# A fixed order of seven slots to a step, and attention by 32x32 tiles summed in PSUM

## The chip, the cores and the metric

The kernel runs on one core of one Trainium2 chip. A core has TensorE (matrix products, into PSUM), VectorE, ScalarE and GpSimd (element-wise work and reductions) and SyncE, which here issues nearly all DMA transfers. Each engine works through its own list of instructions in order and waits on semaphores for the others. The metric is the device time of one execution in microseconds (us), given as the median of several runs. One execution is also recorded by the hardware profiler; its page and trace are what is read below. In the profile PE is TensorE's matmuls, PEld its weight loads, DVE VectorE, ACT ScalarE, POOL GpSimd, SP SyncE, and a trailing q an engine's sequencer.

## What is computed

The input `x` is 4 x 4096 rows of 512 values in fp32. Three residual stages follow each other:

```python
x = x + 0.5 * ffn(layernorm(x))          # first half
x = x + attention(layernorm(x))          # neighbourhood attention
x = x + 0.5 * ffn(layernorm(x))          # second half, same weights
```

`ffn` is one 512 x 512 linear layer whose input and weight are first quantised in blocks of 32 values: each block is scaled so that its largest magnitude is 7.5 and rounded to the nearest of a six-bit grid. The attention has 16 heads of 32 values. Each query sees the 13 keys around it (fewer offsets at the ends of a sequence, where the window is shifted):

```python
qkv = x @ qkv_w.T + qkv_b                       # q is scaled by 32 ** -0.5
attn = softmax(q . k[neighbours] + rpb[offset]) # 13 scores a query and head
out = (attn . v[neighbours]) @ proj_w.T + proj_b
```

## The kernel before

**Precision.** fp32 products are made from fp16 halves: each operand is a rounded high part and a low part, and the helper `product` (L148-160) sums three groups of matmuls, high x low, low x high and high x high, with four pieces of the contraction each: 12 matmuls of 128x128 weights on 512 columns. An FFN or output product has one more, for the bias (L152).

**Stages of a row tile.** A tile `t` has 128 rows (128 tiles in all). It is loaded (`load`), normalised and quantised (`quantised_norm(t, "n1")`, L187-205), multiplied (`ffn`, L214-221), normalised again (`layernorm`, L170-185), transposed by DMA into `x2`, and its values are computed and written to HBM (`values`, L235-249). The row statistics and the scale factors go over VectorE and GpSimd, `nbn` (L183) on VectorE. Splitting and transposing is in `transposed` (L207-212): ScalarE makes the high half, VectorE the low one, SyncE issues the transposing DMA. After the attention `project_out` (L460-469) multiplies, adds the residual and starts the third norm ("n3"), and `second_half` (L471-473) does the last FFN and stores the tile.

**Stages of an attention item.** An item `m` is four heads (one of four pieces `c` of 128 channels) of a group of four tiles, 512 rows; there are 128 items. Queries are cut into blocks of 30, whose neighbourhoods cover 42 keys; a group has 16 to 18 blocks, 2192 blocks in all over the items. `project_qk` (L280-318) makes queries and keys (2 x 12 matmuls), keeps the last 42 positions of each item in `halo` for the next group (two VectorE copies), and copies each head's queries into a block-diagonal tile `bd`, one copy per head and half (VectorE for three heads, ScalarE for one). `softmax` (L343-399) then needs two matmuls a block, both with 128x128 weights from `bd` (the first gives scores against the high and the low keys at once, 84 columns, the second those of the low queries, 42 columns):

```python
nc.tensor.matmul(o, bd[:, 0, i, :], keys, start=True, stop=False)
nc.tensor.matmul(o[:, 0, :], bd[:, 1, i, :], keys[:, 0, :], start=False, stop=True)
```

The two sets of scores lie apart in PSUM. VectorE adds the bias table to the first (L377) and then the second to that (L380). Then come the maximum (VectorE), its subtraction (GpSimd), the exponential (ScalarE), the sum and its reciprocal (VectorE), the scaling (GpSimd), the split into halves (L394-396) and the transposing DMA into `pT` (L398). `attend` (L401-458) makes one matmul a block, 126x128 weights from the value stack `vs` on 120 columns (four heads of 30 queries); only a quarter of the result is wanted, so ScalarE picks the four heads' pieces out of PSUM into a tile `a` (L445, twelve instructions an item), then copies the high half into `ring` (L454), and VectorE makes the low half (L455). The value stack is loaded from HBM by `load_stack`, for two items at a time.

**What sets the order.** `run_step` (one step for each tile and item, L482-520) calls the stages in a fixed sequence with their offsets in steps, `attend` at a raised priority (`AHEAD`). A scheduler then decides the place of each instruction on each engine from estimated durations and priorities. The setup (weights quantised, split and transposed, bias table) is interleaved with the first four steps. In the last steps (`ending`) work of GpSimd goes to VectorE.

Of the kernel before, what the change touches and what calls it, by code (L numbers as in the profile page):

```python
# [35 lines left out]
P = 128  # L37
# [5 lines left out]
ROWS = 4 * QN  # L43
# [4 lines left out]
PSB = 6  # L48
VB = 8
# [9 lines left out]
AHEAD = 150  # L59
# [6 lines left out]
def macaron_kernel(  # L66
# [27 lines left out]
    ps_m = ctx.enter_context(tc.tile_pool(name="ps_m", bufs=3, space=PSUM))  # L94
    ps_s = ctx.enter_context(tc.tile_pool(name="ps_s", bufs=1, space=PSUM))
    ps_v = ctx.enter_context(tc.tile_pool(name="ps_v", bufs=1, space=PSUM))
    xp = ctx.enter_context(tc.tile_pool(name="xp", bufs=15))
# [30 lines left out]
    table = const.tile([ROWS, 3, KC, KN], F32, name="table")  # L128
# [32 lines left out]

    xs, ys = {}, {}
    ending = False
# [6 lines left out]
    def layernorm(t, which):  # L170

        st = sm.tile([P, 6], F32, tag=f"st{which}", name=f"st{which}_{t}")
        nc.vector.bn_stats(st, xs[t])  # L173
        mv = sm.tile([P, 2], F32, tag=f"mv{which}", name=f"mv{which}_{t}")
        nc.vector.bn_aggr(mv, st)  # L175
        rs = sm.tile([P, 1], F32, tag=f"rs{which}", name=f"rs{which}_{t}")
        nc.gpsimd.tensor_scalar(  # L177
            rs, mv[:, 1:2], XS ** -2, LN_EPS * XS ** -2, ALU.mult, ALU.add
        )
        nc.gpsimd.tensor_tensor(rs, rs, minus_half, ALU.pow)  # L180
        y = yp.tile([P, dim], F32, tag=f"y{which}", bufs=2 if which == "n1" else 1, name=f"y{which}_{t}")
        nb = sm.tile([P, 1], F32, tag=f"nb{which}", name=f"nb{which}_{t}")
        nc.vector.scalar_tensor_tensor(nb, mv[:, 0:1], -1.0, rs, ALU.mult, ALU.mult)  # L183
        nc.scalar.activation(y, xs[t], AF.Identity, bias=nb, scale=rs)  # L184
        return y

    def quantised_norm(t, which):  # L187

        y = layernorm(t, which)
# [8 lines left out]
        eng = nc.vector if ending else nc.gpsimd  # L198
        eng.tensor_tensor(yb, yb, bc(r, QB), ALU.mult)  # L199
        q8 = q8p.tile([P, dim], F8, tag=f"q8{which}", name=f"q8_{which}_{t}")  # L200
        nc.scalar.activation(q8, y, AF.Identity, bias=nudge, saturate=False)  # L201
        eng.tensor_tensor(yb, blocks(q8), bc(sc, QB), ALU.mult)  # L202
        xT = xtp.tile([P, 2, KC, P], F16, tag=f"xT{which}", name=f"xT{which}_{t}")
        transposed(y, xT.rearrange("p s c q -> p (s c) q"), which, t)
        ys[t] = xT

    def transposed(y, dst, which, t):  # L207

        hl = hlp.tile([P, 2, dim], F16, tag=f"hl{which}", name=f"hl{which}_{t}")
        nc.scalar.copy(hl[:, 0, :], y)  # L210
        nc.vector.tensor_tensor(hl[:, 1, :], y, hl[:, 0, :], ALU.subtract)  # L211
        nc.sync.dma_start_transpose(out=dst, in_=hl.rearrange("p s k -> p (s k)"))

    def ffn(t, which):  # L214
# [5 lines left out]
        )  # L220
        nc.vector.scalar_tensor_tensor(xs[t], pm, cf, xs[t], ALU.mult, ALU.add)  # L221

    def first_half(t):

        ffn(t, "f1")
        y = layernorm(t, "n2")
        g, i = divmod(t, GROUP)
        if i == 0:
            x2[g] = x2p.tile([P, 2, KC, GROUP, P], F16, tag="x2", name=f"x2_{g}")
        transposed(y, x2[g][:, :, :, i, :].rearrange("p s c q -> p (s c) q"), "n2", t)  # L230
# [4 lines left out]
    def values(t):  # L235
# [7 lines left out]
        product(pm, lambda s, c: xg[:, s, c, i, :], lambda s, c: wt[:, s, c, VO : VO + dim])  # L243
        vt = vtp.tile([P, 2, dim], F16, tag="vt", name=f"vt{t}")
# [14 lines left out]
    def kind(j):  # L259
        return 1 if j == 0 else 2 if j == n_blocks - 1 else 0  # L260

# [18 lines left out]
    def project_qk(m):  # L280
# [5 lines left out]
        if g > 0:  # L286
            nc.vector.tensor_copy(t[:, :, :, :KN], halo[:, c])
        for s in (0, 1):
            pm = ps_m.tile([P, GT], F32, tag="mm", name=f"pmqk{s}_{m}")
            o = (QO, KO)[s] + c * P  # L290
# [4 lines left out]
            )  # L295
            bias = qk_b[:, s, c : c + 1]
            nc.scalar.activation(t[:, s, 0, KN:], pm, AF.Identity, bias=bias)
            nc.vector.scalar_tensor_tensor(  # L298
                t[:, s, 1, KN:], pm, bias, t[:, s, 0, KN:], ALU.add, ALU.subtract
            )  # L300
        if g + 1 < NG:
            nc.vector.tensor_copy(halo[:, c], t[:, :, :, GT:])
        if c == KC - 1:
            del x2[b * NG + g]

        j0, j1 = group_blocks[g]
        regular = j1 - j0 - (1 if j1 == n_blocks else 0)
        at = KN + j0 * QN - g * GT
        for h in range(4):
            rows = slice(h * D, (h + 1) * D)  # L310
            (nc.scalar.copy if h == 0 else nc.vector.tensor_copy)(  # L311
                bd[rows, :, :regular, h * QN : (h + 1) * QN],
                t[rows, 0, :, at : at + regular * QN].rearrange("p s (n q) -> p s n q", q=QN),
            )
            if j1 == n_blocks:
                nc.vector.tensor_copy(
                    bd[rows, :, regular, h * QN : (h + 1) * QN], t[rows, 0, :, KN + GT - QN :]
                )
# [24 lines left out]
    def softmax(m):  # L343
# [6 lines left out]
        ps = ps_s.tile([P, 3, 2, 256], F32, tag="s", name=f"ps{m}")  # L350
        for i in range(n):
            k0 = KN + span(j0 + i)[1] - g * GT
            u, w = divmod(i, PSB)
            o = ps[:, u, :, w * KN : (w + 1) * KN]
            keys = t[:, 1, :, k0 : k0 + KN]
            nc.tensor.matmul(o, bd[:, 0, i, :], keys, start=True, stop=False)
            nc.tensor.matmul(o[:, 0, :], bd[:, 1, i, :], keys[:, 0, :], start=False, stop=True)

        def pieces(i, e):

            while i < e:
                u, w = divmod(i, PSB)
                whole = max((e - i) // PSB, 1) if w == 0 else 1
                f = min(e, (u + whole) * PSB)
                yield slice(u, u + whole), slice(w, w + (f - i) // whole)
                i = f

        sf = sfp.tile([ROWS, MAXB, KN], F32, tag="sf", name=f"sf{m}")
        s4 = sf.rearrange("p (u w) k -> p u w k", w=PSB)
        p4 = ps[:ROWS, :, :, : PSB * KN].rearrange("p u a (w k) -> p a u w k", k=KN)  # L370
        first = 1 if kind(j0) == 1 else 0
        last = n - (1 if kind(j1 - 1) == 2 else 0)
        for i, e in ((0, first), (first, last), (last, n)):
            for u, w in pieces(i, e):
                o = s4[:, u, w, :]
                bias = table[:, kind(j0 + i), c, :].unsqueeze(1).unsqueeze(1).to_broadcast(o.shape)
                nc.vector.tensor_tensor(o, p4[:, 0, u, w, :], bias, ALU.add)  # L377
        for u, w in pieces(0, n):
            o = s4[:, u, w, :]
            nc.vector.tensor_tensor(o, o, p4[:, 1, u, w, :], ALU.add)  # L380
        s = sf[:, :n, :]
        top = sm.tile([ROWS, MAXB], F32, tag="top", name=f"top{m}")
        nc.vector.tensor_reduce(top[:, :n], s, AX.X, ALU.max)
        eng = nc.vector if ending else nc.gpsimd
        eng.tensor_tensor(s, s, bc(top[:, :n], KN), ALU.subtract)  # L385
        nc.scalar.activation(s, s, AF.Exp, scale=alpha[:ROWS])
        total = sm.tile([ROWS, MAXB], F32, tag="total", name=f"total{m}")
# [3 lines left out]
        eng.tensor_tensor(s, s, bc(total[:, :n], KN), ALU.mult)  # L391
        p = p_tile
        ph = p[:ROWS, :n, :KN]
        nc.scalar.copy(ph, s)  # L394
        nc.vector.tensor_copy(p[:ROWS, :n, 2 * KN : KV], ph)
        eng.tensor_tensor(p[:ROWS, :n, KN : 2 * KN], s, ph, ALU.subtract)
# [4 lines left out]
    def attend(m):  # L401
# [7 lines left out]
        a = ap.tile([P, MAXB * QN], F32, tag="a", name=f"a{m}")  # L409
        for i0 in range(0, n, VB):  # L410
            i1 = min(i0 + VB, n)
            k = i1 - i0
            pv = ps_v.tile([P, 2, 512], F32, tag="v", name=f"pv{m}_{i0}")
            for i in range(i0, i1):
                u, w = divmod(i - i0, VB // 2)
                nc.tensor.matmul(  # L416
                    pv[:, u, w * ROWS : (w + 1) * ROWS], st[:KV, i, col : col + P], pT[:KV, i, :ROWS],
                    start=True, stop=True,
                )
            full = k == VB  # L420
            assert full or k <= VB // 2
            pieces = [(i0, i1, 0)]
            if j1 == n_blocks and i1 == n:
                assert not full
                pieces = [(i0, n - 1, 0)] if n - 1 > i0 else []
                pieces.append((n - 1, n, n_blocks * QN - length))
            for h in range(4):
                rows = slice(h * D, (h + 1) * D)
                for e0, e1, skip in pieces:
                    w0 = e0 - i0  # L430
                    if full:
                        src = pv[rows, :, : VB // 2 * ROWS].rearrange(
                            "p u (w r) -> p u w r", r=ROWS
                        )[:, :, :, h * QN : (h + 1) * QN]
                        dst = a[rows, e0 * QN : e1 * QN].rearrange(
                            "p (u w q) -> p u w q", u=2, q=QN
                        )
                    else:
                        src = pv[rows, 0, w0 * ROWS : (w0 + e1 - e0) * ROWS].rearrange(
                            "p (w r) -> p w r", r=ROWS  # L440
                        )[:, :, h * QN + skip : (h + 1) * QN]
                        dst = a[rows, e0 * QN : e1 * QN - skip].rearrange(
                            "p (w q) -> p w q", q=QN - skip
                        )
                    nc.scalar.activation(dst, src, AF.Copy, scale=1.0 / PS)  # L445
        t0 = b * length + j0 * QN
# [378 lines left out]
```

## Time and profile before

| | |
|---|---|
| Median of 3 runs | 2903.63 us (2900.07 to 2906.81) |
| Profiled execution | 2901.23 us, its span 2899.4 us |
| VectorE busy | 2514.7 us, 87% of the span, 5212 instructions |
| TensorE busy | 2464.3 us, 85%, 16195 matmuls |
| ScalarE busy | 1821.8 us, 63%, 3570 |
| GpSimd busy | 1447.8 us, 50%, 1675 |
| Mean busy share of the 16 DMA engines, 1000-2000 us | 0.65, 123 GB/s |
| Mean granted TensorE clock | 0.955 of full speed |

The time of an engine is the time in which at least one of its instructions was running. Durations of matmuls overlap, since they are pipelined, so the distance between two starts says more than the mean duration. The page's groups give, for each line of the kernel, the operation, its tiles and shapes, the count, the busy time and mean of one, and after a bar the idle time of the engine just before it with what ended that.

### The profile page before, as it was taken

Reading aid. Unit: us, or ns where it says so; the run is one execution under the profiler, and the core shown is the slowest. Engines: PE = TensorE matmul, PEld = TensorE weight load, DVE = VectorE, ACT = ScalarE, POOL = GpSimd, SP = SyncE. Lnnn points to the kernel's source line nnn. Section 1 sums busy time; section 2 is a strip of 40 time slices with the busy share of each in tenths; the row PEclk is TensorE's granted clock in tenths of the full one; section 3 lists DMA queues with packets and bytes.
Section 4 is the critical chain, followed back from the end, with each engine's and each line's share of the span. In section 5 each row is a group of like instructions: output and inputs, shape, how many; then the busy total and the mean of one; then the engine's idle time right before and its main releaser. Section 6 shows DMA issues by size and latency. Waiting matters only on the chain.

```text
span 2899.4 us, 47348 instructions
## 1 busy us (share of the span) xinstructions
PE 2464.3 (85%) x16195; PEld 1217.8 (42%) x16195; DVE 2514.7 (87%) x5212; ACT 1821.8 (63%) x3570; POOL 1447.8 (50%) x1675
## 2 busy tenths in 40 slices
PE   1689998889898889888888888889888888888997
PEld 0244444444444434444444444344444444444443
DVE  8788988998889988888888988898888898889896
ACT  4466666666666666666665666566666566666664
POOL 5344554555455555555554555455555454545540
PEclk9899999999999999999999999999999999999998
DMA  7756765765765766766667665666666766658663
GB/s 199 161 96 121 132 124 113 137 127 110 136 127 117 136 123 120 133 119 121 132 125 124 122 123 112 127 120 121 129 121 124 126 122 126 119 110 143 127 110 78
DMA packets 931326, 362.01 MB, mean 125 GB/s; under 512 B 722830, under 2 KB 893706, under 8 KB 931084
## 3 DMA queue, kind: packets, MB, share of 16 engines
q1 hardware_dynamic: 931024, 358.98, 64.7%
q8 instruction: 127, 2.08, 0.3%
q14 instruction: 115, 0.94, 0.1%
q10 hardware_dynamic: 60, 0.01, 0.0%
HBM read 113.81 MB, written 67.27 MB: 62 GB/s over the span
## 4 chain that ended last, share of the span: by engine, by line
DVE 41%; DMA 25%; PE 11%; issue 9%; POOL 7%; ACT 6%; SPq 2%; DVEq 0%; POOLq 0%; ACTq 0%
DMA x<-in_L_attn_x_dram 9%; DVE bd L311 6%; DVE hln L211 5%; PE pmf L157 5%; DMA out_dram<-x 5%; DMA pT<-p 5%; DMA xTn<-hln 4%; DVE qk L298 4%; DVE scn L192 3%; DVE stn L173 3%; DVE x L221 2%; ACT a L445 2%; DVE scn L193 2%; DVE nbn L183 2%; POOL yn L202 2%
## 5 line engine op out<-in xcount | busy, mean ns | idle before, releaser
L157 PE MATMUL pmf<-wt,xTn 128*128 128x512 f16 x3072 | 755.0, 394 | 87.4 <-DMA xTn<-hln 82.0
L157 PE MATMUL pmqk<-x,wt 128*128 128x512 f16 x3072 | 725.8, 386 | 19.2 <-DVE vt L246 12.1
L184 ACT ACTIVATE yn<-x,nbn,rsn 128x512 f32<-128x512 f32 x384 | 310.2, 811 | 420.5 <-DVE nbn L183 412.8
L445 ACT ACTIVATE a<-pv 32x240 f32<-32x240 f32 (+2 forms) x1536 | 456.7, 301 | 136.0 <-PE pv L416 121.0
L157 PEld LDWEIGHTS <-xTn 128*128 128x128 f16 x3072 | 304.2, 101 | 481.4 <-DMA xTn<-hln 95.9
L157 PEld LDWEIGHTS <-wt 128*128 128x128 f16 x3072 | 300.5, 99 | 374.6 <-issue 48.1
L177 POOL TENSOR_SCALAR rsn<-mvn 128x1 f32<-128x1 f32 x384 | 112.1, 292 | 656.4 <-DVE mvn L175 517.1
L157 PE MATMUL pmv<-wt,x 128*128 128x512 f16 x1536 | 370.4, 392 | 34.3 <-DMA x<-hln 34.2
L173 DVE BATCH_NORM_STATS2 stn<-x 128x6 f32<-128x512 f32 x384 | 264.2, 689 | 136.1 <-DMA x<-in_L_attn_x_dram 131.8
L211 DVE TENSOR_TENSOR hln<-yn,hln 128x512 f16<-128x512 f32 x384 | 334.2, 871 | 46.4 <-ACT hln L210 45.5
L157 PE MATMUL pmo<-wt,ring 128*128 128x512 f16 x1536 | 369.0, 383 | 4.9 <-ACT ring L454 4.9
L199 POOL TENSOR_TENSOR yn<-yn,rn 128x512 f32<-128x512 f32 x248 | 269.9, 1092 | 187.1 <-DVE rn L197 135.6
L210 ACT CAST hln<-yn 128x512 f16<-128x512 f32 x384 | 236.4, 616 | 153.2 <-POOL yn L202 106.7
L416 PE MATMUL pv<-pT,vs 126*128 126x120 f16 x2192 | 183.3, 222 | 159.4 <-DMA pT<-p 126.9
L202 POOL TENSOR_TENSOR yn<-q_n,scn 128x512 f32<-128x512 fp8e4 x248 | 277.5, 1126 | 72.9 <-ACT q_n L201 72.9
L385 POOL TENSOR_TENSOR sf<-sf,top 120x714 f32<-120x714 f32 (+2 forms) x126 | 181.1, 1437 | 232.9 <-DVE mvn L175 108.1
L391 POOL TENSOR_TENSOR sf<-sf,total 120x714 f32<-120x714 f32 (+2 forms) x126 | 178.8, 1419 | 195.2 <-DVE total L390 125.1
L201 ACT ACTIVATE q_n<-yn,nudge 128x512 fp8e4<-128x512 f32 x256 | 184.0, 720 | 127.0 <-POOL yn L199 119.6
L221 DVE SCALAR_TENSOR_TENSOR x<-pmf,coef,x 128x512 f32<-128x512 f32 x256 | 184.9, 726 | 78.5 <-PE pmf L157 76.7
L416 PEld LDWEIGHTS <-vs 126*128 126x128 f16 x2192 | 144.7, 100 | 234.0 <-issue 150.9
L311 DVE COPY bd<-qk 32x1020 f16<-32x1020 f16 (+2 forms) x384 | 235.2, 612 | 7.6
L180 POOL TENSOR_TENSOR rsn<-rsn,minus_half 128x1 f32<-128x1 f32 x384 | 217.4, 566 | 30.7
(126 smaller groups left out, 3847.1 us busy)
## 6 DMA issues: line engine op xcount, KB each, us to landing
vs<-vd SPq DMA_DIRECT2D x144, 357.0 KB
x<-in_L_attn_x_dram SPq DMA_DIRECT2D x128, 256.0 KB
vd<-vt SPq DMA_DIRECT2D x128, 256.0 KB
out_dram<-x SPq DMA_DIRECT2D x128, 256.0 KB
vs<-vd SPq DMA_DIRECT2D x24, 378.0 KB
vs<-vd SPq DMA_DIRECT2D x24, 315.0 KB
xTn<-hln SPq DMA_TRANSPOSE x256
norm_of<-in_L_attn_qkv_w_dram SPq DMA_DIRECT2D x12, 256.0 KB
```

The costliest lines, as they stand in the source:

```text
L157: nc.tensor.matmul(pm, lhs(a, c), rhs(b, c), start=(n == 0), stop=(n == last))
L173: nc.vector.bn_stats(st, xs[t])
L180: nc.gpsimd.tensor_tensor(rs, rs, minus_half, ALU.pow)
L184: nc.scalar.activation(y, xs[t], AF.Identity, bias=nb, scale=rs)
L199: eng.tensor_tensor(yb, yb, bc(r, QB), ALU.mult)
L202: eng.tensor_tensor(yb, blocks(q8), bc(sc, QB), ALU.mult)
L210: nc.scalar.copy(hl[:, 0, :], y)
L211: nc.vector.tensor_tensor(hl[:, 1, :], y, hl[:, 0, :], ALU.subtract)
L221: nc.vector.scalar_tensor_tensor(xs[t], pm, cf, xs[t], ALU.mult, ALU.add)
L311: (nc.scalar.copy if h == 0 else nc.vector.tensor_copy)(bd[rows, :, :regular, h * QN : (h + 1) * QN], t[rows, 0, :, at : at + regular * QN ...
L416: nc.tensor.matmul(pv[:, u, w * ROWS : (w + 1) * ROWS], st[:KV, i, col : col + P], pT[:KV, i, :ROWS], start=True, stop=True,)
L445: nc.scalar.activation(dst, src, AF.Copy, scale=1.0 / PS)
```

## The change

The queue orders, the form of the attention and some places of work change; the computation of the 75 large matmuls of a step stays as it is.

*Order.* The stages become generators. A table of slots holds what begins when; `yield n, rank` in a stage says that its next part belongs `n` slots later, at that rank within the slot. The program is written slot by slot under `manual_schedule`, in which each engine keeps the written order. A step is seven slots. `run_step`, `AHEAD` and `ending` go away; the whole setup is written ahead of the slots. PSUM buffers for large products become four instead of three, buffers of `x` 19 instead of 15.

```diff
+    slots = {}
+    def begin(slot, stage, rank=5):
+        slots.setdefault(slot, []).append((rank, stage))
+    def run_slot(slot):
+        for _, stage in sorted(slots.pop(slot, ()), key=lambda e: e[0]):
+            for n, rank in stage:
+                begin(slot + n, stage, rank)
+                break
...
+    STEP = 7
+    F1, V, QK, SC, PV, OUT, F2 = 6, 2 * STEP + 1, 5 * STEP + 3, 6 * STEP + 5, 8 * STEP + 5, 13 * STEP + 2, 15 * STEP
...
+    for t in range(NT):
+        k = t * STEP
+        begin(k - 15, one(load, t), 0)
+        begin(k - 5, quantised_norm(t, "n1"), 1)
+        begin(k + F1, first_half(t))
+        begin(k + V, values(t))
+        begin(k + OUT, project_out(t))
+        begin(k + F2, second_half(t))
+    for m in range(n_items):
+        k = m * STEP
+        begin(k + QK, project_qk(m))
+        begin(k + SC, softmax(m), 6)
+        begin(k + PV, attend(m))
...
+        begin(k + 6 * STEP, one(load_stack, b, g, 0), 9)
+        begin(k + 8 * STEP, one(load_stack, b, g, 1), 9)
```

So within a step the slots hold, in turn: f2; values; output; queries; keys; `pv` and then the scores; f1. A norm's parts (statistics, factors, normalising, scales, first product on GpSimd, rounding, second product, high half, low half with its transposing DMA) stand in one slot each, nine in all, and the product that needs the transpose three slots after the last.

*Scores.* `bd` goes away. Each head's queries and keys are read where they lie, on the 32 partitions of the head; a matmul has weights of 32x32 and 42 columns, and writes the 32 partitions of its head. The three products of halves are summed in PSUM, so one addition of the table is left. The rows of a block become 32 for 30 queries.

```diff
-            nc.tensor.matmul(o, bd[:, 0, i, :], keys, start=True, stop=False)
-            nc.tensor.matmul(o[:, 0, :], bd[:, 1, i, :], keys[:, 0, :], start=False, stop=True)
+            for k, (a, e) in enumerate(((0, 1), (1, 0), (0, 0))):
+                for h in range(4):
+                    rows = slice(h * D, (h + 1) * D)
+                    nc.tensor.matmul(
+                        ps[rows, u, w * KN : (w + 1) * KN],
+                        t[rows, 0, a, q0 : q0 + QR], t[rows, 1, e, k0 : k0 + KN],
+                        start=k == 0, stop=k == 2,
+                    )
...
-            nc.vector.tensor_tensor(o, o, p4[:, 1, u, w, :], ALU.add)
```

*Values.* Each head has a matmul of its own, 126x32 weights on 30 columns, which writes the head's 32 partitions; the results of an item lie side by side in PSUM and are read as they are. The tile `a` goes away.

```diff
+            for h in range(4):
                 nc.tensor.matmul(
-                    pv[:, u, w * ROWS : (w + 1) * ROWS], st[:KV, i, col : col + P], pT[:KV, i, :ROWS],
+                    pv[h * D : (h + 1) * D, u, w * QN : (w + 1) * QN],
+                    st[:KV, i, col + h * D : col + (h + 1) * D],
+                    pT[:KV, i, h * QR + r : h * QR + r + QN],
                     start=True, stop=True,
                 )
...
-                    nc.scalar.activation(dst, src, AF.Copy, scale=1.0 / PS)
...
-            nc.scalar.copy(rh, piece)
-            nc.vector.tensor_tensor(ring[:, 1, c, r : r + e - t0], piece, rh, ALU.subtract)
+            nc.scalar.activation(
+                ring[:, 0, c, r : r + k], pv[:, u, at : at + k], AF.Copy, scale=1.0 / PS
+            )
+            nc.vector.scalar_tensor_tensor(
+                ring[:, 1, c, r : r + k], pv[:, u, at : at + k], 1.0 / PS, ring[:, 0, c, r : r + k],
+                ALU.mult, ALU.subtract,
+            )
```

*Places of work.* The two `halo` copies move from VectorE to ScalarE, `nbn` from VectorE to GpSimd; the last steps keep GpSimd's work on GpSimd.

```diff
-            nc.vector.tensor_copy(t[:, :, :, :KN], halo[:, c])
+            nc.scalar.copy(t[:, :, :, :KN], halo[:, c])
-        nc.vector.scalar_tensor_tensor(nb, mv[:, 0:1], -1.0, rs, ALU.mult, ALU.mult)
+        nc.gpsimd.tensor_scalar(nb, mv[:, 0:1], rs, -1.0, ALU.mult, ALU.mult)
```

## The prediction

> **What bounds the kernel now.** I read the engine shares first, then the long groups, then the chain of waits, and last the order of time inside one burst of attention.
>
> ```profile
> PE 2464.3 (85%) x16195; PEld 1217.8 (42%) x16195; DVE 2514.7 (87%) x5212; ACT 1821.8 (63%) x3570; POOL 1447.8 (50%) x1675
> ...
> DVE 41%; DMA 25%; PE 11%; issue 9%; POOL 7%; ACT 6%; SPq 2%; DVEq 0%; POOLq 0%; ACTq 0%
> ...
> L311 DVE COPY bd<-qk 32x1020 f16<-32x1020 f16 (+2 forms) x384 | 235.2, 612 | 7.6
> ```
>
> Two engines are nearly full. The chain that ended last runs 41% on VectorE and 25% on transfers, 11% on TensorE: now one, now the other is late. The third line is work that serves only the form of the attention: the block-diagonal copy of the queries, 235.2 us of VectorE.
>
> What does TensorE need? In 1500-1523 us twelve products in a row take 2.75 us with the last counted at its own 0.38, so 2.37 / 11 = 0.2155 us from start to start. A step has 75 of 512 columns (13 + 13 for the two FFNs, 12 values, 24 queries and keys, 13 output): 75 x 0.2155 = 16.16 us. The attention's are in the order of time:
>
> ```profile
> 1521.70 0.53 PE L416 MATMUL pv<-pT,vs 126*128 126x120 f16 x7
> 1522.06 0.20 PE L356 MATMUL ps<-qk,bd 128*128 128x84 f16 x1
> 1522.11 0.18 PE L357 MATMUL ps<-qk,bd 128*128 128x42 f16 x1
> 1522.13 0.20 PE L356 MATMUL ps<-qk,bd 128*128 128x84 f16 x1
> ...
> 1522.82 0.20 PE L356 MATMUL ps<-qk,bd 128*128 128x84 f16 x1
> ```
>
> The first column is the start, the second the duration, which overlaps the next. From 1522.06 to 1522.82 lie 12 blocks of two matmuls: 63 ns a block; in the trace's nanoseconds 36.5 for the 84 columns and 25.5 for the 42. A value product (0.53 us for seven, the last at 0.22) is 51.5 ns. With 2192 / 128 = 17.1 blocks a step that is 17.1 x (62 + 51.5) = 1.94 us. So TensorE needs 18.1 us of a step; the stretch 1000-2000 us holds 5782 matmuls, 126.5 a step, so a step takes 21.9. VectorE is busy for 868 of those 1000 us.
>
> **The change, part by part.**
>
> *VectorE.* Gone, by their groups' busy times: `bd` copies 235.2 + 15.4, the second addition of the scores 127 (63.4 + 29.7 + 29.1 + 5.1), the two halo copies 62.5 + 37.6 (to ScalarE), `nbn` 99.2 (to GpSimd): 577 us. The subtraction for `ring` now reads PSUM in about as many pieces (117 us stay). 2514.7 - 577 = 1938 us, 15.1 us a step. It stops being the bound as long as a step is longer.
>
> *ScalarE* loses `bd` (132), most of `a` (457) and gets 224 halo copies (37.6 + 62.5 on VectorE, up to twice that here): below 1400 us. *GpSimd* gets 384 small operations of about 292 ns (the row of L177): 112 us, some 1580 in all. Both hide under TensorE; their cover goes only if a step falls below 12.4 us.
>
> *TensorE.* The 75 products stay. The order of the built program shows, in each step, output, queries and keys, `pv`, `ps`, f1, f2, values. A block becomes 3 x 4 score matmuls of 32x32 on 42 columns and 4 value matmuls of 126x32 on 30 columns: 16 for 3, each with its own weight load, 274 pairs a step. No row of the trace has a tile of 32 columns. Bounds: if the four heads' tiles run side by side and each is as long as the 42-column matmul, 25.5 / 4 = 6.4 ns a pair; if loading and running one tile fill 25.5 each and nothing overlaps, 51 ns. In between stand 51 / 4 = 12.75 (a tile's load and run in sequence, four tiles side by side) and 25.5 (no tile beside another, loads hidden as now). I take 12.75: consecutive heads use other rows of the array and other rows of PSUM, and the trace does show a load hidden under another matmul; but 25.5 is the row nearest to it and is my first rival. 274 x 12.75 ns = 3.49 us.
>
> A skill rule speaks against it: "TensorEngine Tiling (Array Packing)", Instruction Overhead, puts about 60 cycles on every matmul however few its columns, and advises against tiling a dimension that is small; the 25.5 ns of 42 columns, where 84 take 36.5, agree with such a floor. By it the attention would be 274 x 25 ns = 6.9 us (estimate). "TensorE: Matmul & The Clock Gate", Part 3, has matmuls on different tiles start about 4 ns apart, which no run here shows; by that it would be 1.1 us (estimate).
>
> Between `pmqk`, `pv`, `ps` and f1 the form of the matmuls changes three times. If each lets the array run empty, it costs duration less spacing of a 512-column matmul, 379 - 216 = 163 ns: 0.49 us. Bounds 0 and 3 x 0.38 = 1.1.
>
> *Waits.* Each engine's order is now fixed, so whatever stands behind a waiting TensorE instruction waits with it: a late `pT` holds `ps` and all products of the next step, and through them every eviction. A slot is about 20 / 7 = 2.9 us. From the transpose of n1 or n3 to its product lie three slots (8.7 us), from that of `p` to `pv` four (11.6). The longest transposes on the chain of before took 5 to 11.5 us from issue to what they released. Stack loads go out at the end of a slot, ahead of the transposes of `p`. SyncE issues per step x 0.35, three transposes 1.25 each, `p` 2.9, values 0.58, output 0.35, a quarter of 12 stack loads at 0.45: 9.3 us, so it keeps up; and 19 x buffers let the load go 12 slots after the store that frees its buffer (before: 102.8 us of waits for that). I take 0.2 us a step for late transfers; bounds 0 and 2 (a transfer of 10.7 us against 8.7, every step). TensorE's code grows from 32,383 instructions to 89,375, 548 of a step's 700 in one burst; the page's instruction queue moved 16 KB at a time, 127 times, which is one per 256 of them. Two such pieces per burst of 3.5 us are new. Their cost is within the same bound.
>
> *Ends.* Before, TensorE had worked 9.0 + 46.1 us by 145 us, and 49.4 of the last 69.4: 110 us lost. Now the weights stand ahead of nearly all tiles, and a step holds all seven products only after 15. In the first 5.4 steps only f1 and values run: VectorE needs 6.1 us (n1 3.0, f1 0.73, n2 1.73, values 0.68) to TensorE's 25 x 0.2155 = 5.4, so 4 us are lost; and the last tile's n3 passes alone through 12 slots, some 13 us by its operations' durations (0.2 to 1.1 us) and one transpose. 110 + 17 = 127 (bounds 90 and 200).
>
> *Sum.* 16.16 + 3.49 + 0.49 + 0.2 = 20.34 us a step, x 128 = 2604, + 127 = 2731; with the 1.8 us around the profiled span (2901.23 to 2899.4) 2733, taken as **2730** against 2901.23. That run lies 2.4 us under the median of 2903.63, below what can be told apart (0.2% is about what a measurement of this kernel can tell from no change).
>
> **Rivals.**
>
> 1. *Tiles one after another.* 25.5 ns a pair: 6.99 us, a step of 23.84, 3051 + 127 + 2 = 3180. For it: the floor visible at 42 columns. Against: there each matmul covers all rows. It decides from 17.6 ns a pair: (2899.4 - 127) / 128 = 21.66, less 16.85, is 4.81 us for 274. This is the slower side.
> 2. *Fully side by side*, 6.4 ns: 1.75 us, a step of 18.6, 2510; VectorE at 15.1 of 18.6 with dependences would add half a microsecond a step, 2570.
> 3. *Fixed order meets late transfers or late code*: the full 2 us a step, 22.15 x 128 + 129 = 2964. For it: DMA is 25% of the chain and its share of 0.65 rises with shorter steps. Against: three and four slots of room.
> 4. *Load and run in sequence, no overlap*, 51 ns: 13.97 us, a step of 30.8, about 4070. Against: LDWEIGHTS hides at every matmul of before.
>
> That the order isn't what the slots say is excluded by the built order.
>
> **How the numbers follow.** Forecast 0.42 (own range 2640 to 2880: 9 to 17 ns), rival 2 0.20, rival 1 0.20, rival 3 0.10, rival 4 0.08. Faster: 0.42 + 0.20 with nearly all of both, 0.62; within 0.2% 0.03 (between forecast and rival 3); slower 0.35. The range leaves out rival 4, the upper part of rival 1 and the lowest of rival 2: 2540 to 3200.
>
> **What would show it.** Right: VectorE at 1900-2000 us busy, `bd`, `a` and the second addition gone, TensorE ending the chain; `ps` 32x42 starting 10 to 15 ns apart; TensorE's waits for `pT` and `xTn` below 30 us together. Wrong at the tile price: bursts of `pv` and `ps` of 7 us instead of 3.5. Wrong at the waits: idle TensorE of 1 us and more in most steps ahead of `pv` or `pmf`, or gaps inside a burst with nothing that released it, at every 256th instruction. Wrong at VectorE: its share still near 87% while TensorE's falls.

## The result, and the profile after

The changed kernel takes 3227.67 us (median of 4 runs, 3218.85 to 3231.78), the kernel before 2902.01 beside it: a ratio of 1.1115, 95% interval 1.1087 to 1.1144. It is slower by 11%, where 6% faster was forecast; the time lies above the range. The profiled execution has a span of 3223.1 us.

First the page of the changed kernel: engines, the granted clock in 40 slices (tenths), the queue that brings TensorE's code, the chain, and three groups of TensorE. The same two lines, clock and queue, of the kernel before stand behind it.

```profile
PE 2661.6 (83%) x44684; PEld 1295.9 (40%) x44691; DVE 2073.3 (64%) x3957; ACT 1291.0 (40%) x2178; POOL 1567.9 (49%) x2081
...
PEclk9888989988898998998989999898998889889987
...
q8 instruction: 349, 5.72, 0.8%
...
PE 82%; issue 14%; DMA 2%; DVE 1%; POOL 0%; ACT 0%; SPq 0%; ACTq 0%; DVEq 0%; POOLq 0%
...
L156 PE MATMUL pmf<-wt,xTn 128*128 128x512 f16 x3072 | 928.3, 465 | 110.2 <-DMA xTn<-hln 67.7
...
L156 PE MATMUL pmqk<-x,wt 128*128 128x512 f16 x3072 | 683.9, 379 | 0.0
...
L407 PE MATMUL ps<-qk 32*32 32x42 f16 x26304 | 258.2, 184 | 373.8 <-issue 373.8
```

```profile
PEclk9899999999999999999999999999999999999998
...
q8 instruction: 127, 2.08, 0.3%
```

VectorE fell to 64% as planned and left the chain; TensorE ends it alone. But 14% of the chain is "issue", time in which nothing that the profile shows was waited for, and 373.8 us of such idle time stand before the score matmuls. And two groups with the same operation and shape differ: a product for the queries takes 379 ns, one for the FFN 465.

The order of time of one step shows both (start, duration, and in brackets the idle time before):

```profile
1516.25 0.69 PE L472 MATMUL pv<-pT,vs 126*32 126x30 f16 x68
1516.87 1.71 PE L407 MATMUL ps<-qk 32*32 32x42 f16 x190
1522.28 0.32 PE L407 MATMUL ps<-qk 32*32 32x42 f16 x14 [3.69 <-issue]
1522.53 0.61 PE L151 MATMUL pmf<-ffn_bias,ones 128*128 128x512 bf16 x1
1522.93 1.48 PE L156 MATMUL pmf<-wt,xTn 128*128 128x512 f16 x3
```

68 value and 190 score matmuls start within 2.2 us, some 8 ns apart. Then TensorE stands for 3.69 us in the middle of a block, between matmuls that depend on nothing new, and finishes the last 14. The bias matmul after that takes 0.61 us instead of 0.38: the trace records half the clock from 1519.9 to 1526.7 us.

Where the 324 us come from: a step takes 23.66 us instead of 21.90 (both from 1000 to 2000 us), which is 225 us in 128 steps; the other 99 lie at the ends. By step:

| TensorE in a step, us | forecast | measured |
|---|---|---|
| 75 products at full clock | 16.16 | 16.16 |
| 274 small matmuls | 3.49 | 2.2 (8.0 ns each) |
| three changes of form | 0.49 | 0.32 (0.093 + 0.105 + 0.12) |
| idle stretch in the scores | within 0.2 for all waits | 3.1 (130 distances over 0.5 us from start to start, 397 us) |
| products at half clock | - | 1.8 (mean spacing 241 ns instead of 216) |
| sum | 20.34 | 23.6 |

The idle stretches have an address. I counted TensorE's instructions from the start of the trace: between 400 and 3000 us lie 124 idle stretches over 0.26 us (111 in the scores, 13 in the FFN product right behind them), and all 124 end at the same place in the count, 189 or 190 past a multiple of 256. Within a burst the place varies: the stretches in the scores come after 73 to 211 of the burst's score matmuls. The queue named "instruction" moves 349 packets of 16 KB, one for each 256 of the 89,375 instructions, and the last packet before TensorE went on had begun 2.2 to 3.4 us earlier (median 2.5). No two of its packets begin less than 3.2 us apart, in any kernel of this study; in the kernel before, the closest two are 10.3 us apart.

### The profile page after: what moved, and what is told of

Same layout as the page of the kernel before. It is cut to its first block, busy times and chain, and to the rows that moved or that the text cites. A ratio compares the mean times of both kernels' runs of the same rounds, so it can differ in the third digit from the quotient of the medians.

```text
span 3223.1 us, 101741 instructions
## 1 busy us (share of the span) xinstructions
PE 2661.6 (83%) x44684; PEld 1295.9 (40%) x44691; DVE 2073.3 (64%) x3957; ACT 1291.0 (40%) x2178; POOL 1567.9 (49%) x2081
## 4 chain that ended last, share of the span: by engine, by line
PE 82%; issue 14%; DMA 2%; DVE 1%; POOL 0%; ACT 0%; SPq 0%; ACTq 0%; DVEq 0%; POOLq 0%
PE pmf L156 27%; PE pmqk L156 21%; PE pmv L156 10%; PE pmo L156 10%; PE ps L407 8%; PE pv L472 2%; PE pmf L151 2%; DMA xTn<-hln 1%; PE pmo L151 1%; DMA norm_of<-in_L_attn_qkv_w_dram 0%; DVE hln L213 0%; DVE stn L185 0%; DMA parts_of<-in_L_attn_qkv_w_dram 0%; DVE x L519 0%; POOL yn L238 0%
## 5 line engine op out<-in xcount | busy, mean ns | idle before, releaser
L156 PE MATMUL pmf<-wt,xTn 128*128 128x512 f16 x3072 | 928.3, 465 | 110.2 <-DMA xTn<-hln 67.7
L156 PE MATMUL pmqk<-x,wt 128*128 128x512 f16 x3072 | 683.9, 379 | 0.0
L156 PEld LDWEIGHTS <-xTn 128*128 128x128 f16 x3072 | 354.4, 116 | 638.4 <-issue 350.0
L407 PE MATMUL ps<-qk 32*32 32x42 f16 x26304 | 258.2, 184 | 373.8 <-issue 373.8
L285 ACT CAST vt<-pmv 128x512 f16<-128x512 f32 x128 | 74.9, 585 | 986.0 <-PE pmv L156 986.0
L407 PEld LDWEIGHTS <-qk 32*32 32x32 f16 x26304 | 230.6, 90 | 391.0 <-issue 387.2
L430 DVE TENSOR_TENSOR sf<-ps,table 128x504 f32<-128x504 f32 (+5 forms) x288 | 126.2, 484 | 321.9 <-PE ps L407 321.9
L344 ACT ACTIVATE qk<-pmqk,qk_b 128x512 f16<-128x512 f32 x256 | 175.8, 687 | 317.9 <-PE pmqk L156 317.9
L196 POOL TENSOR_TENSOR rsn<-rsn,minus_half 128x1 f32<-128x1 f32 x384 | 248.7, 648 | 31.9
L348 DVE SCALAR_TENSOR_TENSOR qk<-pmqk,qk_b,qk 128x512 f16<-128x512 f32 x256 | 190.9, 746 | 63.9 <-ACT qk L344 63.9
```

Source lines behind the costliest of these rows:

```text
L156: nc.tensor.matmul(pm, lhs(a, c), rhs(b, c), start=(n == 0), stop=(n == last))
L348: nc.vector.scalar_tensor_tensor(t[:, s, 1, KN:], pms[s], bias, t[:, s, 0, KN:], ALU.add, ALU.subtract)
L407: nc.tensor.matmul(ps[rows, u, w * KN : (w + 1) * KN], t[rows, 0, a, q0 : q0 + QR], t[rows, 1, e, k0 : k0 + KN], start=k == 0, stop=k == 2,)
```

## The experiments

**Theory A.** TensorE's code arrives in pieces of 256 instructions, with at most one piece ahead, and a piece takes some 4 us to come (an estimate: the 2.9 us of the median stretch, and about 1 us in which the burst ran through the piece before). A burst of 548 instructions at 4 ns each outruns it. The idle stretch in turn halves the clock for the products behind it. **Theory B**, the rival: both belong to the tile matmuls, an idle cost for so many of them and too little work to hold the clock. Ten kernels were run. Small edits were made to the changed kernel, except where another is named. Kernels 2, 3, 4 and 5 were run once, the others four or five times.

**1. The scores in three pieces, each behind a product.**

```diff
         for i in range(n):
+            if i in (6, 12):
+                yield 1, 6
...
-        yield 1, 9
+        yield 2, 9
...
-    ... SC, PV ... = ... 6 * STEP + 5, 8 * STEP + 5
+    ... SC, PV ... = ... 6 * STEP + 2, 8 * STEP + 5
```

> The scores of an item are cut into three pieces of up to 6 blocks, one behind the output, one behind the query and one behind the key products; the value matmuls stay in their slot. Number and form of all matmuls stay. Theory A (code supply: TensorE's code comes in pieces of 256 instructions, the next is asked for when the one before is entered, and a burst of 548 instructions uses them up faster than they come; the half clock follows the idle stretch): no burst holds more than 144 small instructions, so the 2.9 us of idle in the scores go to below 0.3 us a step and the half-clock stretches with them; a step is 16.2 + 2.1 + four changes of form at 0.22 = 19.2 us, 2590 us in all, 2550 to 2680. Theory B (the idle time belongs to the tile matmuls themselves, so many ns for each, and they are too small to hold the clock up): the same 272 tile matmuls cost the same idle time and clock wherever they stand: 3150 to 3300 us.

Measured: 2655.11 us, ratio 0.9115 (0.9084 to 0.9145). Its page, and one step of its order of time:

```profile
PE 2493.2 (94%) x44691; PEld 1229.8 (46%) x44691; DVE 2150.4 (81%) x3957; ACT 1271.0 (48%) x2178; POOL 1579.8 (60%) x2081
...
PE 93%; DMA 2%; DVE 2%; issue 1%; POOL 1%; ACT 0%; SPq 0%; ACTq 0%; DVEq 0%; POOLq 0%
```

```profile
1512.77 0.73 PE L409 MATMUL ps<-qk 32*32 32x42 f16 x72
1513.42 2.76 PE L156 MATMUL pmqk<-x,wt 128*128 128x512 f16 x12
1516.12 0.73 PE L409 MATMUL ps<-qk 32*32 32x42 f16 x72
1516.78 2.76 PE L156 MATMUL pmqk<-x,wt 128*128 128x512 f16 x12
1519.47 0.73 PE L409 MATMUL ps<-qk 32*32 32x42 f16 x72
1520.13 0.92 PE L474 MATMUL pv<-pT,vs 126*32 126x30 f16 x68
```

The same matmuls, the same number of instructions, no bracket: idle time between score matmuls is down from 397 to 8 us (15 us more now lie between value matmuls, where there had been none), and the time at half clock from 630 to 105 us (262 before the change). "issue" falls from 14% of the chain to 1%. A step takes 19.32 us. Theory B expected 3150 at least and is out.

**2. Fewer score matmuls in one burst.**

```diff
-            for k, (a, e) in enumerate(((0, 1), (1, 0), (0, 0))):
+            for k, (a, e) in enumerate(((0, 0),)):
...
-                        start=k == 0, stop=k == 2,
+                        start=True, stop=True,
```

> The scores are made of the high halves alone (one matmul a block and head instead of three; the two products with low halves are left out). The burst has 272 instructions instead of 548. Theory A: the piece that is running and the one already there hold 256 to 512 instructions, so only some 6 in 100 bursts wait: idle time inside the scores below 30 us in all; a step is 16.2 + 1.1 + 0.3 = 17.6 us, with VectorE at 16.2 the next bound: 2380 to 2480 us. Theory B: idle time falls by the number of score matmuls to a third, about 125 us, and the half clock stays in a third of it: 2600 to 2700 us.

Measured: 2463.49 us, one idle stretch of 2.6 us in the scores, 122 us at half clock. The burst is whole but short enough, as A says; by B a third of the idle time had to stay.

**3. A burst of 408 instructions.**

```diff
-        yield 1, 9
+        yield 3, 9
...
-    ... SC, PV ... = ... 6 * STEP + 5, 8 * STEP + 5
+    ... SC, PV ... = ... 6 * STEP + 3, 8 * STEP + 5
```

> The scores move two slots ahead, behind the query product, so that the key product stands between them and the value matmuls; the scores' burst has 408 instructions, the values' 136. Theory A: a burst of 408 finds the rest of the running piece and the next one, so it waits in about 6 of 10 steps (when less than 152 of the running piece are left), and the values' burst hardly ever: idle time in the scores 200 to 260 us instead of 374, in all 2950 to 3080 us. Theory B: all of the idle time lay in the scores and their number stays: 374 us and 3200 to 3260 us.

Measured: 2947.3 us, just below what A expected, with 64 stretches in the scores, 162 us in all, also below A's 200 to 260: half of the 128 bursts wait where 59 in 100 were expected. The groups of this kernel by shape say more:

```profile
L156 PE MATMUL pmqk<-x,wt 128*128 128x512 f16 x3072 | 814.8, 421 | 25.2 <-issue 22.6 <-DVE scn L226 2.6
L156 PE MATMUL pmf<-wt,xTn 128*128 128x512 f16 x3072 | 737.8, 392 | 72.0 <-DMA xTn<-hln 69.9 <-issue 2.0
...
L407 PE MATMUL ps<-qk 32*32 32x42 f16 x26304 | 295.3, 183 | 153.9 <-issue 150.1
```

Now the key product stands behind the scores, and it is now `pmqk` that is slow (421 ns) and `pmf` that is well (392): whatever follows the idle stretch pays for the clock. This kernel also holds both kinds of burst side by side. Of its 64 score bursts with an idle stretch over 0.5 us, 53 had the clock halved within them or in the 6 us behind; of the 64 without one, 6. So it is the idle stretch that goes with the half clock, and the small matmuls without it seldom halve it.

**4. The fixed order undone, the tiles kept.**

```diff
-    with tc.manual_schedule():
-        while slots:
-            run_slot(slot)
-            slot += 1
+    while slots:
+        run_slot(slot)
+        slot += 1
```

> The same stages in the same written order, but the scheduler may again move instructions on each engine (the fixed order is undone, the tiles stay). Theory A: where it puts products between the small matmuls the idle time goes, so less than 374 us inside the scores and attention; where it leaves the bursts whole it stays at 374. Theory B: the idle time stays at about 374 us whatever the order. If the fixed order itself were what costs, this would be back near 2900 us; if not, within 3000 to 3250 us.

Measured: 3149.94 us, 134 stretches, 375 us. The scheduler left the bursts whole, so the stretches stay: they don't come from the fixed order. It says little else, since a kernel bound by this can't show what an order is worth.

**5. An idle stretch put in by hand.** This is kernel 1 with f1's bias matmul reading a copy of the ones that ScalarE rewrites after each eviction of the values.

```diff
+        nc.scalar.copy(late_ones, ones.unsqueeze(1).to_broadcast([P, 16, P]))
...
-            pm, lambda s, c: xT[:, s, c, :], lambda s, c: wt[:, s, c, FO : FO + dim], ffn_bias
+            pm, lambda s, c: xT[:, s, c, :], lambda s, c: wt[:, s, c, FO : FO + dim], ffn_bias,
+            late_ones[:, 0, :] if which == "f1" else ones,
```

> The spread kernel (scores in three pieces) with an idle stretch of TensorE put in by hand, and no other change of its matmuls: the bias matmul of f1 reads a tile of ones that ScalarE rewrites after the eviction of the values, so TensorE stands about 3 us (0.85 + about 2.2) in every step. Theory A (the half clock follows the idle stretch): half-clock time goes from about 105 us to 400 us or more, the f1 and f2 products that come after are slower, and the time is 2655 + 128 x (3 + 1.5 to 2.2): 3180 to 3350 us. Theory B (the half clock came from the 32x32 matmuls in one burst): half-clock time stays near 105 us and only the idle time is added: 2990 to 3060 us.

Measured: 3139.62 us. Its order of time, and 1000 to 2000 us of its stretches (busy times, then the granted clock, DMA share and GB/s):

```profile
1504.53 0.69 PE L477 MATMUL pv<-pT,vs 126*32 126x30 f16 x68
1507.81 0.39 PE L153 MATMUL pmf<-ffn_bias,late_ones 128*128 128x512 bf16 x1 [2.59 <-ACT late_ones L507]
1508.04 2.75 PE L158 MATMUL pmf<-wt,xTn 128*128 128x512 f16 x12
```

```profile
1000.00:2000.00 1000.00, 885.28 (x15045) 426.28 (x15044) 685.78 (x1286) 485.73 (x755) 522.12 (x687) 0.94 0.64 118
```

The same stretch of kernel 1 has a clock of 1.00 and 18006 matmuls. 120 waits, 330 us from value matmul to f1 where there had been 16, bring the time at half clock from 105 to 439 us. The sum closes: 2655 + 314 + (439 - 105) / 2 = 3136. The time is below the range that A gave, since the wait came out at 2.6 us and not 3; the step shown even escaped the half clock, as 23 of the 120 did. An idle stretch in each step is enough to bring the half clock back in most of them. That short matmuls ahead of it play no part is not shown, because 1.2 us of them stand before the wait here too; kernel 3 shows only that by themselves they seldom halve it.

**6. Two pieces of nine blocks instead of three of six**, again from kernel 1.

```diff
-            if i in (6, 12):
+            if i == 9:
...
-    ... SC ... = ... 6 * STEP + 2
+    ... SC ... = ... 6 * STEP + 3
```

> As the spread kernel, but the scores in two pieces of nine blocks (216 instructions each), behind the query and the key products. Theory A: each burst is still below 256 instructions, so no idle time; one change of form and back less in a step, 0.09 + 0.12 us: 128 x 0.21 = 27 us less than 2655, about 2628 (2610 to 2650). Rival: two bursts of 216 with only one product of 2.6 us between them use the code up faster than it comes: idle time of 0.5 us and more a step, 2700 us or more.

Measured: 2754.79 us, ratio 0.9451 (0.9424 to 0.9479). A miss of mine: I had counted each burst by itself, and what I had written as the rival (2700 or more) is what came. Its order of time:

```profile
1507.64 2.76 PE L156 MATMUL pmqk<-x,wt 128*128 128x512 f16 x12
1510.34 1.14 PE L409 MATMUL ps<-qk 32*32 32x42 f16 x96
1511.41 0.69 PE L474 MATMUL pv<-pT,vs 126*32 126x30 f16 x68
1512.03 0.39 PE L151 MATMUL pmf<-ffn_bias,ones 128*128 128x512 bf16 x1
1512.26 0.59 PE L156 MATMUL pmf<-wt,xTn 128*128 128x512 f16 x2
1514.73 2.33 PE L156 MATMUL pmf<-wt,xTn 128*128 128x512 f16 x10 [1.88 <-issue]
```

In this step the wait falls into f1, three large matmuls after the burst. In all 51.7 us of such waits lie in the values, 17.9 in the scores and 15.6 in the FFN products; from 145 to 2600 us 68 of the 69 waits over 0.26 us lie at one place of this kernel's count modulo 256. From the first small matmul at 1506.54 to that point are some 575 instructions in 6.3 us, a piece in 2.8; kernel 1 asks for one in 3.3 us (616 instructions in 7.9) and hardly waits. So the rate over a few microseconds counts, and not only the length of one burst; the packets, never less than 3.2 us apart, fit that. The waits (85 us instead of 23) and the half clock (163 us instead of 105) make up some 90 of the 127 us by which my 2628 was missed; the rest stays open.

**7. The fixed order with block-diagonal scores.** The 32x32 scores are undone, the rest stays: `bd` and its copies come back (one head on ScalarE, three on VectorE), and the scores are still summed in PSUM, three matmuls a block.

```diff
-                for h in range(4):
-                    rows = slice(h * D, (h + 1) * D)
-                    nc.tensor.matmul(
-                        ps[rows, u, w * KN : (w + 1) * KN],
-                        t[rows, 0, a, q0 : q0 + QR], t[rows, 1, e, k0 : k0 + KN],
-                        start=k == 0, stop=k == 2,
-                    )
+                nc.tensor.matmul(
+                    ps[:, u, w * KN : (w + 1) * KN], bd[:, a, i, :], t[:, 1, e, k0 : k0 + KN],
+                    start=k == 0, stop=k == 2,
+                )
```

> The slots stay, the values' tiles stay, but the scores are made as before the change, with block-diagonal weights of 128x128 (copies on VectorE and ScalarE come back), though summed in PSUM: three matmuls of 42 columns a block in place of twelve. The burst has 51 + 68 pairs, 238 instructions. Theory A (code supply and idle time): no burst needs a second new piece, so idle time inside it below 30 us and half clock near 105 us; TensorE needs 16.2 + 17.1 x 3 x 25.5 ns + 0.54 + 0.33 = 18.3 us a step, VectorE 2150 + 235 = 2385 us or 18.6 a step: 2560 to 2700 us. So it would show that the fixed order, not the 32x32 scores, brings the gain. Rival: without the tiles VectorE is the bound again and the fixed order gives little: 2800 to 2900 us.

Measured: 2611.67 us, ratio 0.8965 (0.8938 to 0.8991). Its page:

```profile
PE 2400.1 (92%) x24963; PEld 1180.5 (45%) x24963; DVE 2402.6 (92%) x4405; ACT 1409.3 (54%) x2306; POOL 1615.6 (62%) x2082
...
DVE 78%; PE 11%; issue 6%; DMA 3%; POOL 1%; ACT 1%; SPq 0%; ACTq 0%; DVEq 0%; POOLq 0%
```

Faster than kernel 1, with VectorE back at the end of the chain; one distance of 0.8 us inside the bursts and 118 us at half clock, as A expected. Twelve tiles at 8 ns take 96 ns a block, three wide matmuls 76: on TensorE the 32x32 scores save nothing. They save the copies, and the kernel that pays for the copies is 43 us faster than the one that deals out the tiles.

**8 and 9. The copies dealt out**: two, then three heads on ScalarE, in kernel 7.

```diff
-            (nc.scalar.copy if h == 0 else nc.vector.tensor_copy)(
+            (nc.scalar.copy if h < 2 else nc.vector.tensor_copy)(
```

The other has `h < 3`; in both the order of the four calls over the three slots changes too, so that the one or two left on VectorE come at another place.

> The block-diagonal kernel in slots, with the copies of two heads on ScalarE instead of one. There VectorE was busy 92% and ended the chain (78%). If VectorE is what bounds it: 96 to 128 copies of 0.62 us go from VectorE, 79 us, and the time falls by 60 to 80: 2530 to 2550 us. Rival (TensorE and the late transposes are already as near as VectorE): 10 to 30 us less, 2580 to 2600 us.

> The same with the copies of three heads on ScalarE. VectorE would need 2402 - 157 = 2245 us, 17.5 a step, less than TensorE's 18.3, so TensorE becomes the bound: a step of 18.6 to 18.9 us, 2490 to 2540 us. Rival (ScalarE, with 1.04 us a copy, holds up evictions of PSUM and so TensorE): 2560 us or more.

Measured: 2537.81 us (0.8713, 0.8696 to 0.8730) and 2529.75 us (0.8688, 0.8672 to 0.8704). With the first TensorE has taken the end of the chain (85%), so the second brings little more. This is the page of the second, the fastest kernel here that computes all of it (kernel 2 leaves products out):

```profile
PE 2379.1 (94%) x24963; PEld 1182.4 (47%) x24963; DVE 2109.4 (83%) x4149; ACT 1676.9 (66%) x2562; POOL 1656.3 (66%) x2082
...
PE 90%; DMA 4%; DVE 3%; ACT 1%; issue 1%; POOL 1%; SPq 0%; ACTq 0%; DVEq 0%; POOLq 0%
```

**10. Kernel 7 with the fixed order undone**, by the edit of experiment 4.

> The block-diagonal kernel with the fixed order undone: the scheduler may move instructions. It tells what the fixed order is worth where no burst is long. If the order is worth what separates the kernel before from it, the time goes back to 2800 us or more; if the gain came from the work taken off VectorE and ScalarE, it stays within 2600 to 2680 us.

Measured: 3010.79 us, ratio 1.0340 (1.0317 to 1.0362). With the same work, the order is worth 399 us. The waits of this kernel name where (who waits for whom, us, times, longest):

```profile
PE pmqk L156 <- DVE x L254: 310.0, 141, 4.7
...
DVE stn L185 <- DMA x<-in_L_attn_x_dram: 193.4, 105, 5.6
```

TensorE waits for the eviction of an FFN product by VectorE. That VectorE is late with it because of waits such as the second line's is my reading and not shown. The stages' written order was made for fixed slots, so this is the worth of the order for this text, not of a scheduler in general: the kernel before, written for one, is at 2902.

## Why the prediction was wrong

*What bounds the kernel now*: right. Work taken off VectorE and a better order do bring the time down; kernels 1, 7 and 9 show it.

*VectorE, ScalarE, GpSimd*: VectorE 2073 us instead of 1938, ScalarE 1291 (below 1400), GpSimd 1568 (1580). All stayed hidden under TensorE, as said. VectorE's difference is one of counting: its instructions overlap at their edges (durations add up to 2833 us before, 2515 are busy). Added up, they fell by 606 us, more than my 577; the busy time fell by 441 only.

*The price of a tile*: I took 12.75 ns; it is 8.0, half the matmuls within 5 to 9 ns of each other, the side of rival 2. The Trainium skill's rule of about 60 cycles for each matmul ("TensorEngine Tiling (Array Packing)", Instruction Overhead), which at 25 ns stood beside my first rival, doesn't hold here for matmuls on different tiles; it does hold for the block-diagonal ones on 42 columns, 25.5 ns in the traces of the kernel before and of kernel 7.

*Changes of form*: 0.32 us instead of 0.49. Each of the three does cost spacing; that the array runs empty there is not shown.

*Waits*: late transfers were harmless in the steps, as said (`pv` waited 2.7 us for `pT` instead of 126.9). My sign of less than 30 us for `pT` and `xTn` together still failed: `xTn` cost 67.7 us, all of it ahead of 126 us and behind 3120. **The step that failed is the sentence on code**: "Their cost is within the same bound." I named the two pieces per burst and then let them share a bound of 2 us that came from transfers, and a value of 0.2. They cost 3.1 us a step. The row was there (127 packets for 32,383 instructions, one per step of 22 us); what I didn't do is ask how long a piece takes to come and set it against the 1 us in which a burst uses one up. The sign of being wrong that I did name, gaps inside a burst with nothing that released them, is what the trace shows.

*The clock* wasn't in the sum at all: 1.8 us a step. The trace of before shows the rule, only at other places: of its windows of 3.4 us in which products held less than a tenth of the time, all 21 at full clock were followed by a half-clock one; of those with at least 40%, none was (counted from 145 us on; in the changed kernel it is 83 of 93, and none of 527).

*Ends*: 3223 - 128 x 23.66 = 194 us instead of 127; kernels 1 and 9 have 181 and 197, so it isn't the idle stretches. I had taken the losses of before, and up to 145 us they are the same (TensorE worked 10.0 + 44.3 us against 9.0 + 46.1). What I had too small is the end: I took 13 us for the last tile alone, but from 3124 us on, where of each step only the output product and f2 are left, TensorE waits for `xTn` eight times, 38.5 us in all, and f2 runs at half clock (12 products in 5.3 us instead of 2.75). By my reading a slot is then too short, at 13.6 us a step, for three of them to cover the transpose.

*The rivals*: rival 1 gave 3180 and the result is 3227, yet its reason was wrong: the tiles cost a third of its price. Rival 3 had the reason (late code), with 2 us a step where 3.1 of idle time and 1.8 of half clock came. A time that fits a rival doesn't make the rival true; the distance between two starts does, and it was to be read off in one line.

## What to carry to other kernels

Count instructions, not only their time: a burst whose code is used up faster than it comes stands still, and the sign is an "issue" gap between instructions that depend on nothing new, always at the same place in the instruction count. Deal small matmuls out among large ones, so that code comes at an even rate and TensorE never idles long enough to lose its clock. A form that saves copies by making many small instructions should first be priced against moving the copies to an idle engine: that beat it here by 125 us (2655 to 2530).

## What the runs showed of the hardware

- TensorE's code came in packets of 16 KB, one for each 256 instructions, and in none of the twelve traces did two begin less than 3.2 us apart. 616 instructions in 7.9 us went by nearly without a wait, 575 in 6.3 us did not, and a burst of 548 instructions at 4 ns waited 2.9 us (median). "Runtime: NRT & Kernel Launch", Instruction fetch mechanics, calls the cost of a crossing mostly hidden, which held in the kernel before and in kernels 7 to 9, whose waits lie at no one place of the count, and not in the changed kernel (397 us).
- Matmuls on the tiles of four heads in turn (32x32 scores, 126x32 values), each with its weight load, started 8 ns apart on average.
- Going from a product to tiles added 93 ns to the spacing, from tiles to a product some 117 ns in all.
- Added idle stretches of about 2.6 us a step made the granted clock one half for 334 us more; the records of the clock change in steps of 3.4 us. In kernel 3, 53 of 64 bursts with an idle stretch and 6 of 64 without one had the clock halved.
